# Second graph attention on four quarters of the matmul array, two tiles at a time, in a float32 GAT layer

## The chip, the cores and the metric

The kernel runs on one core of a Trainium2 chip. The metric is the device time of one execution in microseconds (us). I quote the median of a kernel's timed runs and, in brackets, the lowest and highest. A profile's span is some 2 us shorter than the device time of the same run, because it goes from the first to the last instruction.

Engines: PE is TensorE (matmul), PEld its weight loads, DVE VectorE, ACT ScalarE, POOL GpSimd, and SP SyncE, whose queue issues nearly all DMA transfers here. L272 means line 272 of that kernel's source.

## The reference

128 batches of 64 nodes with 512 features go through a graph attention layer with four heads, a second attention with one head, a feed-forward block and two norms. The part concerned here is the second attention and what follows it.

```python
def _gat_heads(x, adj, W, a):                     # x: [B, N, F]
    Wh = einsum('bnf,hfo->bhno', x, W)
    f1 = einsum('bhno,ho->bhn', Wh, a[:, :O])
    f2 = einsum('bhno,ho->bhn', Wh, a[:, O:])
    e = f1[:, :, :, None] + f2[:, :, None, :]
    e = where(e > 0, e, 0.01 * e)
    e = where(adj > 0, e, -1e9)
    return einsum('bhnm,bhmo->bhno', softmax(e), Wh)

# h = relu(layernorm(x)), then, with B = 128, N = 64, F = O = D = 512, H = 4:
h = elu(_gat_heads(h, adj, W_heads, a_heads))     # four heads, joined to [B, N, 2048]
out = elu(_gat_heads(h, adj, W_out, a_out))       # the second attention
y = maximum(out @ w1 + b1, 0) @ w2 + b2 + out
return x + layernorm(y) * gamma + beta
```

Each batch attends only within itself: the second attention is, for each batch, a 64x64 matrix times a 64x512 matrix.

## The kernel before

A tile is 128 partitions, that is two batches of 64 nodes, by 512 features. Four tiles form a group, and there are 16 groups. The large products run as seven half-size products each instead of eight (Strassen's scheme, in `unit`). Work of neighbouring groups is interleaved, so that TensorE always has a product to do. Cuts are marked with `# ...`.

The PSUM pools: six banks for products, two (`aux`) for everything else. The buffers for x tiles: four, shared by the x that the next group needs (`x`) and the x for the residual of a finished group (`xr`). Both are issued on the SP queue, as are the weights and the stores of results.

```python
    def bank(name):
        return ps.tile([P, 2, T], FP, tag="mm", name=name)        # 6 buffers

    def aux(shape, name):
        return ps.tile(shape, FP, tag="aux", name=name, bufs=2)

    def load(t, name="x"):
        tl = wk.tile([P, F], FP, tag="x", name=f"{name}{t}", bufs=4)
        nc.sync.dma_start(out=tl, in_=xf[ts(t, P), :])
        return tl
```

The second attention. `softmax2` leaves its weights as a block-diagonal 128x128 matrix for each tile (the two off-diagonal quarters are zero), so that one full matmul does both batches of a tile:

```python
    def transpose_weights2(g):
        # ... AT2[g][:, j, :] is the transposed block-diagonal matrix of tile j
    def attend2(g, j):
        pa = aux([P, FO], f"pa2_{g}_{j}")
        nc.tensor.matmul(pa, AT2[g][:, j, :], WH2[g][:, j, :], start=True, stop=True)
        # ...
        elu(OUT[g][:, j], pa, f"2_{g}_{j}")

    def elu(dst, src, name):
        ex = wk.tile([P, 512], FP, tag="elu", name=f"ex{name}", bufs=3)
        nc.scalar.activation(ex, src, AF.Relu, scale=-1.0)
        nc.scalar.activation(ex, ex, AF.Exp, scale=-1.0)
        nc.vector.scalar_tensor_tensor(dst, ex, -1.0, src, ALU.add, ALU.max)
```

The end of a tile's way: the residual is loaded, the norm taken, the result stored.

```python
        def finish(j):
            t = G * g + j
            xr = load(t, "xr")
            nc.gpsimd.tensor_tensor(xr, xr, bs, ALU.add)
            y = o[:, j]
            mean, rstd = norm_stats(y, "n2", t)
            nc.vector.scalar_tensor_tensor(y, y, mean, gs, ALU.subtract, ALU.mult)
            nc.vector.scalar_tensor_tensor(y, y, rstd, xr, ALU.mult, ALU.add)
            nc.sync.dma_start(out=of[ts(t, P), :], in_=y)
```

The seven products of a unit run in the order 1, 5, 6, 2, 3, 7, 4. Product 7 accumulates into the bank of product 6, so it may begin only when VectorE has added product 1 to that bank (L272) and ScalarE has copied the sum away (L273):

```python
        own = {1: 1, 2: 1, 5: 5, 3: 5, 6: 6, 7: 6, 4: 6}
        def after(p):
            if p in (1, 5, 6):
                nm = {1: "s1", 5: "s5", 6: "t"}[p]
                sb[nm] = wk.tile([P, 2, T], FP, tag=nm, name=f"{nm}_{name}")
                if p == 6:
                    nc.vector.tensor_tensor(gb[6], gb[6], sb["s1"], ALU.add)   # L272
                nc.scalar.copy(sb[nm], gb[p])                                  # L273
                # ...
```

And the first norm of a later group's tiles starts on VectorE with the statistics of x (L343), which have to wait for x's DMA:

```python
    def norm_stats(src, tag, t):
        st = sm.tile([P, 6], FP, tag=tag + "st", name=f"{tag}st{t}")
        nc.vector.bn_stats(st, src)                                            # L343
        # ...
    def norm1(t):
        if t not in X:
            X[t] = load(t)
        mean, rstd = norm_stats(X[t], "n1", t)
        # ...
```

## Time and profile before

| | before |
|---|---|
| device time, us | 2364.29 (2364.02 to 2364.80), 3 runs |
| length of each steady group, us | 142.96 |
| second attention on TensorE | 128 instructions of 592 ns, 0.86 us from start to start for a tile |
| SP queue's transfers of x, xr, results | 66, 64 and 64 of 256 KB |
| x, from issue to landing | 3.6 us (median) |

The prediction below shows the span, the busy times and the timeline of the second attention. First, what the SP queue issued around the start of a group (start in us, duration in us, queue, line, operation, destination<-source, count):

```profile
329.43 1.13 SPq L750 DMA_DIRECT2D out_dram<-o  x2
330.65 0.91 SPq L238 DMA_DIRECT2D w<-tc  x2
331.65 0.86 SPq L95 DMA_DIRECT2D x<-in_x_dram  x2
```

Read it as a queue: two stores, two weights, then two x tiles. The tiles' transfers landed at 335.25 and 335.94. Then the same moment on the engines (timeline of all engines, start in us, duration in us; in brackets the idle time before and what ended it):

```profile
335.57 1.28 DVE L343 BATCH_NORM_STATS2 n1st<-x 128x6 f32<-128x512 f32 x2
...
336.98 1.89 PE L307 MATMUL g_a<-zs_z,w 128*128 128x256 f32 x8
...
338.98 0.70 DVE L272 TENSOR_TENSOR g_a<-g_a,s_a 128x512 f32<-128x512 f32 x1 [1.72 <-PE g_a L307]
...
339.77 0.59 ACT L273 COPY t_a<-g_a 128x512 f32<-128x512 f32 x1 [1.95 <-DVE g_a L272]
```

The statistics of x were done by 336.9, before the sum of L272 was wanted: VectorE sat idle for 1.72 us ahead of it and then started the sum as soon as TensorE's product 6 was complete. Product 7 was not delayed. This group had the most room: over the twelve steady groups the idle time ahead of the sum was 0.14 to 1.72 us.

### The profile page before, as it was taken

How to read it: one execution, taken by the hardware profiler on the slowest of the kernel's cores; microseconds unless marked ns; L12 is line 12 of the kernel's file. 1: busy time of each engine (PE TensorE's matmuls, PEld its weight loads, DVE VectorE, ACT ScalarE, POOL GpSimd, SP SyncE). 2: the span in 40 equal slices, each digit the busy share in tenths (PEclk: the TensorE clock that was granted, in tenths of full speed). 3: DMA queues.
4: the chain of work that ended last, by engine and by line, in shares of the span. 5: the costliest groups of instructions: out<-in, count | busy, mean ns of one | idle time of the engine just before them, and what ended most of it. 6: DMA issues, size and time to landing. Idle time of an engine off the chain costs nothing.

```text
span 2360.4 us, 32849 instructions
## 1 busy us (share of the span) xinstructions
PE 2317.9 (98%) x11805; PEld 1934.5 (82%) x11805; DVE 1265.5 (54%) x2210; ACT 911.0 (39%) x1623; POOL 1026.7 (43%) x917
## 2 busy tenths in 40 slices
PE   6989999999999999999999999999999999999997
PEld 4868787888878888787887878888788887878885
DVE  7625474554646556474554745556464563744527
ACT  2524425253352533425244251533525344251513
POOL 5664444416344353443524444253443534533333
PEclk7999999999999999999999999999999999999999
DMA  8545353444535445353444544435354453534443
GB/s 308 184 142 193 125 183 127 164 152 132 182 125 178 134 139 179 126 180 129 154 163 129 182 131 161 153 130 181 127 177 132 138 179 127 182 118 164 157 148 106
DMA packets 257809, 366.89 MB, mean 155 GB/s; under 512 B 22216, under 2 KB 145128, under 8 KB 257648
## 3 DMA queue, kind: packets, MB, share of 16 engines
q1 hardware_dynamic: 251024, 343.82, 43.9%
q0 software_dynamic: 4512, 16.78, 1.9%
q10 hardware_dynamic: 2112, 4.19, 0.5%
q8 instruction: 95, 1.56, 0.3%
q14 instruction: 66, 0.54, 0.1%
HBM read 337.45 MB, written 27.26 MB: 155 GB/s over the span
## 4 chain that ended last, share of the span: by engine, by line
PE 94%; DVE 2%; ACT 1%; POOL 1%; issue 0%; DMA 0%; DVEq 0%
PE g_b L322 33%; PE g_a L307 32%; PE g_c L307 8%; PE g_d L322 8%; PE pz L525 4%; PE pa L673 2%; PE pto L700 1%; PE pzS L525 1%; PE pth L371 1%; PE s1pt L472 1%; PE pf L381 1%; PE s1pe L406 1%; DMA x<-in_x_dram 0%; PE s2pt L667 0%; PE pwa L193 0%
## 5 line engine op out<-in xcount | busy, mean ns | idle before, releaser
L322 PE MATMUL g_b<-w,h 128*128 128x256 f32 x2560 | 598.1, 381 | 0.0
L322 PEld LDWEIGHTS g_b<-w,h 128*128 128x128 f32 x2560 | 480.5, 190 | 72.2 <-issue 10.1
L307 PE MATMUL g_a<-z,w 128*128 128x256 f32 x1520 | 361.0, 380 | 1.2 <-DVE g_a L581 0.7
L307 PE MATMUL g_a<-zs_z,w 128*128 128x256 f32 x1504 | 347.9, 379 | 0.0
L307 PEld LDWEIGHTS g_a<-z,w 128*128 128x128 f32 x1520 | 287.6, 190 | 57.9 <-issue 14.3
L307 PEld LDWEIGHTS g_a<-zs_z,w 128*128 128x128 f32 x1504 | 284.8, 190 | 50.5 <-issue 14.3
L322 PE MATMUL g_b<-w,hS 128*128 128x256 f32 x1024 | 243.5, 382 | 0.0
L585 POOL TENSOR_TENSOR hS<-hS,h 128x512 f32<-128x512 f32 x64 | 83.0, 1297 | 366.8 <-DVE hS L549 366.8
L547 ACT ACTIVATE exc<-g_a 128x512 f32<-128x512 f32 x256 | 152.3, 595 | 199.7 <-DVE g_a L581 119.6
L322 PEld LDWEIGHTS g_b<-w,hS 128*128 128x128 f32 x1024 | 191.4, 191 | 30.9 <-issue 6.7
L549 DVE SCALAR_TENSOR_TENSOR h<-exc,g_a 128x512 f32<-128x512 f32 x192 | 131.6, 686 | 136.3 <-ACT exc L548 136.2
L548 ACT ACTIVATE exc<-exc 128x512 f32<-128x512 f32 x256 | 161.6, 631 | 6.5
L615 POOL TENSOR_TENSOR h<-h,h 128x512 f32<-128x512 f32 x64 | 86.7, 1362 | 138.1 <-PE g_b L322 138.0
L332 POOL TENSOR_TENSOR zs_z<-zS,z 128x512 f32<-128x512 f32 x63 | 89.7, 1424 | 128.3 <-PE g_a L307 123.7
L615 POOL TENSOR_TENSOR h<-hS,h 128x512 f32<-128x512 f32 x64 | 81.1, 1268 | 142.4 <-PE g_b L322 142.4
L474 ACT COPY at<-s1pt 128x512 f32<-128x512 f32 x64 | 34.7, 588 | 279.8 <-PE s1pt L472 279.8
L307 PE MATMUL g_c<-ot,w 128*128 128x256 f32 x512 | 123.9, 385 | 0.8 <-DVE n2ve L347 0.8
L322 PE MATMUL g_d<-w,rt 128*128 128x256 f32 x512 | 121.5, 380 | 1.7 <-DVE o L740 1.0
L307 PE MATMUL g_a<-zS,w 128*128 128x256 f32 x496 | 117.2, 379 | 0.0
L639 DVE SCALAR_TENSOR_TENSOR jf<-wh,ao 128x512 f32<-128x512 f32 x128 | 94.3, 776 | 40.3 <-ACT wh L621 40.1
L333 POOL TENSOR_TENSOR zs_z<-z,zs_z 128x512 f32<-128x512 f32 x63 | 85.4, 1357 | 61.1 <-PE g_a L307 40.7
L307 PEld LDWEIGHTS g_c<-ot,w 128*128 128x128 f32 x512 | 93.9, 190 | 21.8 <-issue 9.3
(159 smaller groups left out, 3535.6 us busy)
## 6 DMA issues: line engine op xcount, KB each, us to landing
w<-tc SPq DMA_DIRECT2D x632, 256.0 KB, 2.6
w<-in_L_gnn_W_heads_dram SPq DMA_DIRECT2D x192, 256.0 KB, 2.7
w<-in_L_gnn_W_out_dram SPq DMA_DIRECT2D x192, 256.0 KB, 2.7
w<-in_L_gnn_w_dram SPq DMA_DIRECT2D x96, 256.0 KB, 2.7
x<-in_x_dram SPq DMA_DIRECT2D x66, 256.0 KB, 3.6
xr<-in_x_dram SPq DMA_DIRECT2D x64, 256.0 KB, 2.8
out_dram<-o SPq DMA_DIRECT2D x64, 256.0 KB, 2.1
tc<-pt POOLq DMA_DIRECT2D x20, 512.0 KB, 5.6
```

Of the source, the lines that this page charges most:

```text
L307: nc.tensor.matmul(bk[:, o, :], w[:, k, ts(o, P)], a[:, k, :], start=start and o == 0 and k == 0, stop=k == 1, skip_group_check=True,)
L322: nc.tensor.matmul(bk[:, j, :], a[:, k, ts(j, P)], w[:, k, :], start=start and k == 0 and j == 0, stop=i == len(ms) - 1 and k == 1, skip_g ...
L332: eng.tensor_tensor(s2, s1, a11, ALU.subtract)
L333: eng.tensor_tensor(s4, a12, s2, ALU.subtract)
L525: nc.tensor.matmul(banks[b][:, c, :].rearrange("p (h n) -> p h n", h=H), src[rows, off + c * P:off + (c + 1) * P], at[rows, b], start=True ...
L547: nc.scalar.activation(ex, src, AF.Relu, scale=-1.0)
L548: nc.scalar.activation(ex, ex, AF.Exp, scale=-1.0)
L549: nc.vector.scalar_tensor_tensor(dst, ex, -1.0, src, ALU.add, ALU.max)
L585: nc.gpsimd.tensor_tensor(dst, dst, H1["22"][:, h], ALU.add)
L615: nc.gpsimd.tensor_tensor(dst[:, h], x0[:, h], x1[:, h], ALU.subtract)
L639: nc.vector.scalar_tensor_tensor(junk, WH2[g][:, j], 1.0, ao[:, c, :], ALU.mult, ALU.mult, accum_out=f[:, c, j:j + 1],)
L673: nc.tensor.matmul(pa, AT2[g][:, j, :], WH2[g][:, j, :], start=True, stop=True)
```

## The change

Half of each full matmul of the second attention multiplies zeros. The change uses only the two diagonal 64x64 quarters, and fills the other two quarters of the array with the second tile: four 64x64 matmuls, one for each of the four batches of two tiles, side by side. A row half of the array writes one PSUM bank, and a column half writes 64 partitions of it. So the results come out as tiles of other pairs of batches: one tile holds the first batch of both tiles, the next one the second batch of both. Everything after is per row and does not care, but the residual must be loaded and the result stored in two halves of 64 partitions (one batch, 128 KB, each), since the two batches of a tile are no longer neighbours in DRAM.

```diff
--- before.py
+++ after.py
@@ -668,22 +668,31 @@
         AT2[g] = wk.tile([P, G, P], FP, tag="hT", name=f"at2_{g}", bufs=4)
         nc.scalar.copy(AT2[g], pt)
 
-    def attend2(g, j):
-        pa = aux([P, FO], f"pa2_{g}_{j}")
-        nc.tensor.matmul(pa, AT2[g][:, j, :], WH2[g][:, j, :], start=True, stop=True)
-        if j == 0:
+    def attend2(g, q):
+
+
+        if q == 0:
             tag = "out" if g < NG - 1 else "z11"
             OUT[g] = big.tile([P, G, FO], FP, tag=tag, name=f"o{g}")
-        elu(OUT[g][:, j], pa, f"2_{g}_{j}")
+        pa = [aux([P, FO], f"pa2_{g}_{q}_{b}") for b in range(NB)]
+        for b in range(NB):
+            rows = slice(b * N, (b + 1) * N)
+            for c in range(2):
+                nc.tensor.matmul(
+                    pa[b][c * N:(c + 1) * N], AT2[g][rows, 2 * q + c, rows],
+                    WH2[g][rows, 2 * q + c, :], start=True, stop=True, skip_group_check=True,
+                )
+        for b in range(NB):
+            elu(OUT[g][:, 2 * q + b], pa[b], f"2_{g}_{q}_{b}")
 
     def stage_e(g):
 
         gap = [lambda: None]
         score = [lambda j=j: scores2(g, j) for j in range(G)]
-        attend = [lambda j=j: attend2(g, j) for j in range(G)]
+        attend = [lambda q=q: attend2(g, q) for q in range(2)]
         return (
             gap + score + [lambda: spread2(g)] + gap * 2 + [lambda: softmax2(g)] + gap * 5
-            + [lambda: transpose_weights2(g)] + gap * 2 + attend[0:2] + gap + attend[2:4] + gap * 3
+            + [lambda: transpose_weights2(g)] + gap * 2 + attend[0:1] + gap * 2 + attend[1:2] + gap * 4
         )
 
 
@@ -740,14 +749,18 @@
             eng.tensor_tensor(dst, a, dst, ALU.add)
 
         def finish(j):
-            t = G * g + j
-            xr = load(t, "xr")
+
+            batches = [NB * (G * g + j // 2 * 2 + c) + j % 2 for c in range(2)]
+            xr = wk.tile([P, F], FP, tag="x", name=f"xr{g}_{j}", bufs=4)
+            for c, b in enumerate(batches):
+                nc.sync.dma_start(out=xr[ts(c, N), :], in_=x[b])
             nc.gpsimd.tensor_tensor(xr, xr, bs, ALU.add)
             y = o[:, j]
-            mean, rstd = norm_stats(y, "n2", t)
+            mean, rstd = norm_stats(y, "n2", G * g + j)
             nc.vector.scalar_tensor_tensor(y, y, mean, gs, ALU.subtract, ALU.mult)
             nc.vector.scalar_tensor_tensor(y, y, rstd, xr, ALU.mult, ALU.add)
-            nc.sync.dma_start(out=of[ts(t, P), :], in_=y)
+            for c, b in enumerate(batches):
+                nc.sync.dma_start(out=out[b], in_=y[ts(c, N), :])
 
         f1 = unit(f"c{g}", product_t(M1, lambda p: bl[1][p]), post1, (1, 5, 6, 2, 3, 7, 4))
         f2 = unit(f"d{g}", product_n([M2], lambda p, i: bl[2][p]), post2, (1, 5, 6, 2, 3, 7, 4))
@@ -839,7 +852,7 @@
             run(ff[2:], [
                 lambda: [scores2(g, j) for j in range(G)], lambda: spread2(g), nothing, nothing,
                 lambda: softmax2(g), *[nothing] * 7, lambda: transpose_weights2(g), nothing,
-                *[lambda j=j: attend2(g, j) for j in range(G)], nothing,
+                *[lambda q=q: attend2(g, q) for q in range(2)], nothing,
             ])
             continue
         early = [lambda: z_sums(g + 1, 0)]
```

## The prediction

> **What bounds the kernel now.** I read the page's first, second and fourth parts, then the waits of TensorE inside the steady part, then the timelines around the second attention and the first attention's scores.
>
> The page: span, busy times, and the chain of work that ended last.
>
> ```profile
> span 2360.4 us, 32849 instructions
> PE 2317.9 (98%) x11805; PEld 1934.5 (82%) x11805; DVE 1265.5 (54%) x2210; ACT 911.0 (39%) x1623; POOL 1026.7 (43%) x917
> ...
> PEclk7999999999999999999999999999999999999999
> ...
> PE 94%; DVE 2%; ACT 1%; POOL 1%; issue 0%; DMA 0%; DVEq 0%
> ...
> PE g_b L322 33%; PE g_a L307 32%; PE g_c L307 8%; PE g_d L322 8%; PE pz L525 4%; PE pa L673 2%; PE pto L700 1%; PE pzS L525 1%; PE pth L371 1%; PE s1pt L472 1%; PE pf L381 1%; PE s1pe L406 1%; DMA x<-in_x_dram 0%; PE s2pt L667 0%; PE pwa L193 0%
> ```
>
> The reader is to see one engine only: TensorE is busy in 98% of the span at full clock and carries 94% of the chain. The waits of TensorE between 250 and 2290 us come back empty, so in fourteen of the sixteen groups of four tiles nothing else ends last. A group lasts 142.96 us (the second attention starts at 796.08 and again at 939.04). There, TensorE time saved is span saved, until something else makes TensorE wait. The changed line, pa at L673, is 2% of the chain: that caps the gain.
>
> The second attention of one group, on TensorE (start in us, length in us, ...). Lengths overlap at the ends; I use start to start.
>
> ```profile
> 937.32 1.89 PE L307 MATMUL g_a<-zs_z,w 128*128 128x256 f32 x8
> 939.04 1.02 PE L673 MATMUL pa<-wh,at 128*128 128x512 f32 x2
> 939.90 1.89 PE L307 MATMUL g_a<-zs_z,w 128*128 128x256 f32 x8
> 941.63 1.02 PE L673 MATMUL pa<-wh,at 128*128 128x512 f32 x2
> 942.49 1.89 PE L307 MATMUL g_a<-z,w 128*128 128x256 f32 x8
> ...
> 947.67 1.02 PE L673 MATMUL pa<-wh,at 128*128 128x512 f32 x2
> 948.53 1.89 PE L307 MATMUL g_a<-zs_z,w 128*128 128x256 f32 x8
> ```
>
> Each float32 matmul is two instructions. One tile's attention takes 939.90 - 939.04 = 0.86 us, i.e. 0.43 us for each 512-column instruction, and lies in the stream of products without any gap. The kernel already has a block of exactly the shape that the change makes, four matmuls on four quarters of the array: the scores of the first attention, 64*64 with 256 columns.
>
> ```profile
> 857.50 1.89 PE L322 MATMUL g_b<-w,h 128*128 128x256 f32 x8
> 859.23 1.89 PE L307 MATMUL g_c<-zs_o,w 128*128 128x256 f32 x8
> 860.95 1.89 PE L322 MATMUL g_b<-w,h 128*128 128x256 f32 x8
> 862.77 1.09 PE L406 MATMUL s1pe<-R,L 64*64 64x256 f32 x16
> 863.80 1.99 PE L307 MATMUL g_c<-ot,w 128*128 128x256 f32 x8
> 865.63 3.62 PE L322 MATMUL g_b<-w,h 128*128 128x256 f32 x16
> 869.08 1.24 PE L322 MATMUL g_d<-w,rt 128*128 128x256 f32 x5
> ```
>
> See that 16 quarter instructions take 1.03 us to the next start, where 16 whole ones take 3.45 (865.63 to 869.08): four run at once. See also what the switch costs: the 8 products ahead last 1.82 us instead of 1.73, and the 8 behind 1.83.
>
> **What the Trainium skill says.** "TensorEngine Tiling (Array Packing)", section Key Properties: tiles work in parallel, but a change of the tiling mode drains TensorE. The trace agrees, with the sum below at 0.37 us for in and out. The same page, Gotcha 1: PSUM Pressure: different row tiles must write to different PSUM banks. The change obeys this (one bank for each half of the rows), and so do the scores above. "TensorE: Matmul & The Clock Gate", Part 3, The mechanism: tiles' matmuls start about 4 ns apart; here the four starts of a set lie 6 to 8 ns apart, hidden all the same.
>
> **The change part by part.**
> 1. Removed from TensorE: 64 whole 128x512 matmuls, 0.86 us each (pa, 128 instructions), 55 us in all. They multiply a block-diagonal matrix whose off-diagonal halves are zero.
> 2. Added: 32 sets of four 64x64 matmuls with 512 columns (256 instructions, so TensorE should have 11,933). Half of a set's products were the zeros. Cost of a set, from the scores: from 860.95 to 865.63 are 4.68 us for 16 whole instructions and 16 quarter ones. Take off 3.45 for the whole ones: 1.23 us remain. Four sets of quarter instructions at the rate of one whole each (3.45/16 = 0.216) are 0.86, so **a switch in and out costs 0.37 us**. The set here has two passes of 512 columns: 2 x 0.43 = 0.86, plus 0.37, is **1.23 us** against 2 x 0.86 = 1.72 for the two tiles that it replaces. Saved: 0.49 us a set, x32 = **15.7 us**. All of it is on the path in the steady groups.
> 3. Unchanged: the ELUs. Two banks of 128x512 come out of a set as out of two tiles before, so 64 Relu of 0.59 us, 64 Exp of 0.63 and 64 VectorE operations of 0.69. Only which batches share a tile is new. ScalarE (39%) and VectorE (54%) keep their load.
> 4. Moved: a set takes both "aux" PSUM buffers at once. By the order of the built program, in a steady group set 1 stands where tile 0 stood, then come four blocks of 8 products (before: pa of tile 1 among them), then set 2, where tile 2 stood.
> 5. DMA: loads of xr and stores of the result become 128 of 128 KB each instead of 64 of 256 KB. Same bytes. Each issue takes the SP queue 0.34 us, so 128 more are 43 us over 2360, in a queue that mostly waits for TensorE to free weight buffers (L238, 655.4 + 529.4 us, the two lines below). Matching each weight load's landing in the trace with the first product that reads it gives 11.5 us at the least in the steady part, 16.3 in the median: hidden.
>
> ```profile
> SPq L238 <- PE g_a L307: 655.4, 434, 8.1
> SPq L238 <- PE g_b L322: 529.4, 371, 9.1
> ```
>
> 6. The tail, where TensorE does wait for others. In the last group the two sets are only one product block (1.73 us) apart, where tiles stood at 2309.69, 2312.28, 2314.86 and 2315.72. Set 2 needs both buffers, so it waits until both ELUs of set 1 are over: about 0.2 to land, then Relu, Exp, Relu, Exp = 2.44 on ScalarE, then 0.69 on VectorE, some 3.4 us from set 1's end, against 1.73. A stall of about 1.7 us. Of this, the later start of set 1 and the shorter sets give part back, and the old chain had its own wait (the fourth ELU ended at 2320.3). By laying these durations end to end I get the last transposed tile copied about 0.9 us later than before. The last store also has one issue more, 0.4 us. Sum: **+1.3 us** (estimate).
>
> Sum: 2364.3 - 15.7 + 1.3 = 2349.9, **2350 us**, a ratio of 1.006.
>
> **The rivals.**
> A. The PSUM buffers become the wait in every group: set 2 waits for set 1's ELUs. For: only two buffers, both taken at once, and ScalarE interleaves other ELUs (before, tile 0's ELU ran from 940.63 to 943.66 with the products' ELUs between). Against: set 2 would start at 939.04 + 1.23 + 4 x 1.73 = 947.2, and the two ELUs end, with the neighbours' work laid between, at about 944.5. Slack 2.6 us. If it did wait by 1 us in each group, the gain would be nil: 2366.
> B. The quarters don't overlap at 512 columns, or the two passes of one float32 matmul run one after another, making some five passes of 0.43 plus 0.37 = 2.5 us a set: +0.8 x 32 = +25, 2390. Against: the scores are issued in the same order (rows outer, columns inner) and overlap fully.
> C. The switch costs less with long passes, because the longer streaming hides the weight loads: at the best 0.86 us a set, -27 us, 2338. Against: half of the 0.37 (0.09 and 0.10) lies in the blocks ahead and behind, where longer passes hide nothing; that leaves some 6 us more at most.
> D. More, smaller DMAs delay weights or the store at the end. Against: 5. above; the worst I can see is 1 to 2 us at the end.
>
> **Range and chances.** The saving of 15.7 rests on a block of like shape measured in the same program, repeated to 0.01 us in each group; I allow it 13 to 18. The tail I allow 0 to 4. So 2345 to 2355. Faster by over 2% needs under 2318, more than all that pa costs less the floor of its passes (C: 2338): chance 0.01. Slower by over 2% needs 2412, beyond B: 0.01. Within 2%: 0.98.
>
> **What would show it right or wrong.** In the changed profile: pa as 64*64 x256; from one product block's start ahead of a set to the second behind it 1.23 us more than the blocks alone (2. right); a group of 141.97 us, 0.98 less than before; no TensorE waits between 250 and 2290 us (A, D wrong); mean length of the four ELU operations as before (3.); at the end one wait of TensorE's pa for VectorE of 1 to 2 us (6.). The prediction is wrong if a wait of pa for VectorE shows in every group (A), or weights' DMAs show as TensorE's releaser (D), or a set takes over 1.7 us (B).

## The result, and the profile after

| us | before | after |
|---|---|---|
| device time, median | 2364.23 (2364.02 to 2364.80), 4 runs | 2354.88 (2350.49 to 2357.07), 4 runs |
| ratio | | 0.9958 (0.994 to 0.9975) |
| device time of the profiled run | 2362.20 | 2357.07 |
| its span | 2360.4 | 2355.3 |

The ratio is the mean time of one kernel's fast runs over that of the other's in the same rounds, so it is not quite the ratio of the medians quoted. (The prediction's 1.006 is the other way round, before over after.) The time is 9.4 us shorter, within 2%; the range of 2345 to 2355 just holds it, but the prediction's middle was 2350.0. And the runs spread over 6.6 us, where those of before spread over 0.8. The profiled run after is the slowest of the four; the profiled run of before is a run apart, 2 us faster than the timed ones.

The page of the changed kernel, first part (span; busy time of each engine, share, instructions):

```profile
span 2355.3 us, 33359 instructions
PE 2306.5 (98%) x11933; PEld 1912.8 (81%) x11933; DVE 1273.8 (54%) x2210; ACT 910.2 (39%) x1623; POOL 1030.3 (44%) x917
```

TensorE lost 11.4 us of busy time, gained the 128 instructions that were expected (11,933), and is still the bound. The sets themselves, in the timeline of TensorE:

```profile
938.12 1.89 PE L307 MATMUL g_a<-zs_z,w 128*128 128x256 f32 x8
939.94 1.09 PE L681 MATMUL pa<-wh,at 64*64 64x512 f32 x8
940.96 1.99 PE L307 MATMUL g_a<-zs_z,w 128*128 128x256 f32 x8
942.79 1.89 PE L307 MATMUL g_a<-z,w 128*128 128x256 f32 x8
```

From 938.12 to 942.79 are 4.67 us; the two blocks of products take 1.73 each, so the set costs 1.22 us, where two tiles cost 1.72. The unrounded starts give 1.217 us for each of the 30 sets outside the last group. A steady group, with two sets, should therefore have shrunk from 142.96 to 141.96 us. To see whether it did, I took the distance between the scores blocks of neighbouring groups. Twelve steady groups have 142.96 us each before. After, they have between 142.02 and 143.19, and their sum is 1711.0 against 1715.5 before and 1703.5 expected: **7.5 us of the 12.0 were lost again**. The waits of TensorE between 250 and 2280 us, a question that had an empty answer before, name where (engine, tile, line, what it waited for: us in total, times, longest):

```profile
PE g_a L307 <- ACT t_a L273: 4.5, 7, 1.0
```

The view counts only idle time that it can see, 4.5 us. The whole 7.5 can be placed with a later run, e5, which has the same 11,933 TensorE instructions in the same order and no such wait: matched instruction by instruction between 250 and 2280 us, all of the extra time (7.4 us) lies ahead of the first two instructions of product 7 of the first head, in each of the twelve groups.

Here is one of these seven, in the timeline of all engines:

```profile
340.91 0.70 DVE L343 BATCH_NORM_STATS2 n1st<-x 128x6 f32<-128x512 f32 x1 [4.25 <-DMA x<-in_x_dram]
...
341.43 1.89 PE L307 MATMUL g_a<-zs_z,w 128*128 128x256 f32 x8
...
341.74 0.66 DVE L343 BATCH_NORM_STATS2 n1st<-x 128x6 f32<-128x512 f32 x1
...
342.73 0.70 DVE L272 TENSOR_TENSOR g_a<-g_a,s_a 128x512 f32<-128x512 f32 x1
...
343.52 0.58 ACT L273 COPY t_a<-g_a 128x512 f32<-128x512 f32 x1 [4.70 <-DVE g_a L272]
...
344.16 0.70 PE L307 MATMUL g_a<-zs_z,w 128*128 128x256 f32 x2 [0.84 <-ACT t_a L273]
```

Read it from the bottom. TensorE stood 0.84 us (product 7 of the first head) for ScalarE's copy, ScalarE for VectorE's sum of L272. VectorE was not waiting for anything just before that sum: it was busy with the statistics of x, which stand ahead of it in its queue and which it had begun only at 340.91, after 4.25 us of waiting for the DMA of x. Before, those statistics were over in time. So the engine named by the wait, ScalarE, is two steps away from the cause. The SP queue shows why x was late:

```profile
331.36 2.42 SPq L763 DMA_DIRECT2D out_dram<-o  x4
333.88 1.30 SPq L238 DMA_DIRECT2D w<-tc  x2
335.28 0.38 SPq L238 DMA_DIRECT2D w<-in_L_gnn_W_heads_dram  x1
335.75 0.89 SPq L95 DMA_DIRECT2D x<-in_x_dram  x2
```

TensorE is 1.0 us later here than before (this run started 2.0 us slower, see below, and one group's sets have saved 1.0). The first store was issued 1.93 us later than before, but the first x load 4.10 us later. The four halves of stores take 2.42 us where the two whole stores took 1.13, and one weight load more stands ahead of x. The tiles' landing, at 340.88 and 341.56, also came 5.1 to 5.3 us after their issue against 3.6 to 3.8 before. Over the whole run, x takes longer from issue to landing (median 3.6 before, 4.1 after), and VectorE's wait for x rose from 110.9 to 153.5 us. Neither total is a measure of the loss, as the experiments show: e5 has 3.9 and loses nothing, e7 waits 151.0 us and loses in one group only.

How late the sum of L272 is decides it. Counted from the scores block of its group, it starts at 48.05 us in every steady group before, and 1.7 to 2.9 us later in every one after. Each group's loss is that lateness less 1.64 us, to within 0.01 us, in all twelve groups: so long a delay is hidden by the products between the sum and product 7, and the rest is paid.

One issue of a half takes the SP queue 0.57 us for stores and 0.55 for residuals (medians of 128 each); whole tiles took 0.34 and 0.38 before.

The tail was expected to hold a wait for the two `aux` buffers. TensorE's timeline of the last group's second set:

```profile
2309.14 1.08 PE L681 MATMUL pa<-wh,at 64*64 64x512 f32 x4
2310.46 1.07 PE L681 MATMUL pa<-wh,at 64*64 64x512 f32 x4 [0.24 <-DVE o L549]
2311.46 1.99 PE L322 MATMUL g_d<-w,rt 128*128 128x256 f32 x8
```

The set came apart by itself: the four instructions that write the first bank went ahead, and the other four waited for the second bank's ELU. The view shows 0.24 us of idle time, because the long overlapping instructions count as busy. From start to start, the set takes 2.32 us to the next block, where one in a steady group takes 1.02: a stall of 1.3 us.

The end of the last VectorE operation and the end of the span lie 3.27 us apart before (2357.15 and 2360.42) and 4.73 after (2350.56 and 2355.30): storing in halves costs 1.5 us at the end.

The first stretches of the program, before any changed instruction, are 2.0 us longer in this profiled run than in that of before: 0.6 us to the first scores block, and 0.7 in each of the next two stretches. They vary by run (the first stretch between scores blocks took 44.9 to 47.9 us over the profiles), and I ascribe them to no part of the change. The page's chain of work broke off near the end of the program in this run, so I don't use it.

### The profile page after: what moved, and what is told of

Read it like the earlier page. It is cut to its first block, busy times and chain, and to the rows that moved or that the text cites. A ratio compares the mean times of both kernels' runs of the same rounds, so it can differ in the third digit from the quotient of the medians.

```text
span 2355.3 us, 33359 instructions
## 1 busy us (share of the span) xinstructions
PE 2306.5 (98%) x11933; PEld 1912.8 (81%) x11933; DVE 1273.8 (54%) x2210; ACT 910.2 (39%) x1623; POOL 1030.3 (44%) x917
## 5 line engine op out<-in xcount | busy, mean ns | idle before, releaser
L307 PE MATMUL g_a<-zs_z,w 128*128 128x256 f32 x1504 | 353.7, 382 | 4.7 <-ACT t_a L273 4.5
L343 DVE BATCH_NORM_STATS2 n1st<-x 128x6 f32<-128x512 f32 x64 | 43.8, 687 | 153.5 <-DMA x<-in_x_dram 153.5
L757 POOL TENSOR_TENSOR xr<-xr,bs 128x512 f32<-128x512 f32 x64 | 89.6, 1402 | 76.1 <-DMA xr<-in_x_dram 48.6
```

The lines of the kernel that those rows point to most:

```text
L307: nc.tensor.matmul(bk[:, o, :], w[:, k, ts(o, P)], a[:, k, :], start=start and o == 0 and k == 0, stop=k == 1, skip_group_check=True,)
```

## The experiments

**The theory (D')**: the sets save what was predicted. Splitting residual loads and stores in halves makes the SP queue late with x, so the statistics of x stand in VectorE's queue when the sum for product 7 is wanted. **The rivals**: the sets themselves disturb the start of a group (other times of the ELUs, both `aux` buffers taken at once), or the loss comes from other work that has moved; then removing the half transfers would not help. Ten kernels were run. Ratios are against the kernel before in the same rounds.

### e1_merged, e3_loads_merged, e4_stores_merged: one transfer for both halves

The changed kernel, with each pair of halves as one DMA over a strided view. e3 does this for the loads alone, e4 for the stores alone.

```diff
-            for c, b in enumerate(batches):
-                nc.sync.dma_start(out=xr[ts(c, N), :], in_=x[b])
+            nc.sync.dma_start(
+                out=xr, in_=x.rearrange("(u c b) n f -> u b c n f", c=2, b=NB)[G // 2 * g + j // 2, j % 2]
+            )
```

> The changed kernel, with each xr load and each store of a result as one transfer of 256 KB over two batches that lie two apart (a strided view of x and out) instead of two of 128 KB. TensorE's and ScalarE's order is that of the changed kernel, line for line; results stay right. Theory D' (the doubled small transfers make the loads of x land later, VectorE's batch statistics wait for them, and the sum g_a+s_a, ScalarE's copy t_a and a TensorE product queue up behind): 2348 to 2350.5 us, no wait of TensorE for ScalarE t_a between 250 and 2280 us, every steady group 141.97 us, spread of runs under 1 us. Rival S (the sets themselves, their ELUs or the PSUM buffers cost the missing time): 2353 to 2357, the t_a waits stay.

> The changed kernel with only the xr loads merged; stores stay split. Theory D': part of the lost time comes back; the four store halves just ahead of the loads of x in the SP queue are the nearer cause, so most waits stay: 2351 to 2355. If loads are the cause: 2349 to 2351.

> The changed kernel with only the stores merged; xr loads stay split. Theory D' with the stores as the nearer cause: 2348.5 to 2351, few or no t_a waits. If loads are the cause: 2353 to 2356.

Measured: e1 2717.9 us (2715.8 to 2719.4), ratio 1.1492; e3 2469.1, ratio 1.0441; e4 2563.5, ratio 1.0841. All three missed their expectation by far (e1 is 353 us slower than the kernel before), and they do not test the question. In e1 the first residual was issued at 263.8 and its reader on GpSimd began at 272.2, 8.4 us later, where a whole tile takes 2.8 from issue to landing before. GpSimd waited 456 us for residuals, and a group took about 165 us. The Trainium skill, "DMA: Bandwidth & Descriptors", section "Why a DMA increments its semaphore by 16 and not by 1", under "How many engines (k)", gives a reason: the number of DMA engines used is the largest one up to 16 that divides the slowest dimension, larger than 1, of both access patterns. My view has a slowest dimension of 2, so it would run on two engines of sixteen. The kept trace of e1 agrees: the semaphore of that first residual got three updates, one 1.0 us after the issue began and two at 272.04 and 272.06, when it landed (one from each engine, as I read it). The same load in the kernel before got sixteen, all at its landing. The largest waits of TensorE in e1 (same question as above; 250 to 2280 us is less of this longer program):

```profile
PE s1pt L472 <- DVE s1A L439: 167.4, 12, 14.2
PE g_a L307 <- ACT t_a L273: 60.4, 12, 5.5
```

The second line is the same wait as in the changed kernel, thirteen times as long in total. Late transfers can reach TensorE by this way, then; by how much the halves do it needs cleaner experiments.

### e2_before_split: the half transfers alone, on the kernel before

Each residual and each result of the kernel before goes in two halves. Nothing else moves: TensorE and ScalarE have the instructions of before in the same order.

```diff
-            xr = load(t, "xr")
+            xr = wk.tile([P, F], FP, tag="x", name=f"xr{t}", bufs=4)
+            for c in range(2):
+                nc.sync.dma_start(out=xr[ts(c, N), :], in_=x[NB * t + c])
...
-            nc.sync.dma_start(out=of[ts(t, P), :], in_=y)
+            for c in range(2):
+                nc.sync.dma_start(out=out[NB * t + c], in_=y[ts(c, N), :])
```

> The kernel before, with only its xr loads and result stores split in two halves of 128 KB (by batches). TensorE's and ScalarE's order is that of the kernel before. Theory D': t_a waits of TensorE appear here too, 2366 to 2372 us (0.2 to 0.6 us in each of twelve groups, plus about 0.4 at the end), and runs spread by some us. Rival S: as before, 2364 to 2365, no waits.

Measured: 2373.9 us (2370.8 to 2375.4), ratio 1.0037. The steady groups grew from 142.96 to between 143.0 and 144.75 us, and the wait that was new after the change is there too, without any set on quarters:

```profile
PE g_a L307 <- ACT t_a L273: 7.6, 9, 1.5
```

The half transfers alone cost 9 us here, a little more than expected. This rules out that the sets are needed for the wait. Matched with the kernel before, instruction by instruction, all of TensorE's extra time between 250 and 2280 us (10.6 us in the profiled run) again lies at product 7.

### e5_old_transfers: the sets alone (wrong results on purpose)

The changed kernel with the transfers of before: each tile loads and stores the two batches that it would have held before. The results are wrong (half the batches land in each other's place); the work on every engine is that of the changed kernel.

```diff
-            batches = [NB * (G * g + j // 2 * 2 + c) + j % 2 for c in range(2)]
-            xr = wk.tile([P, F], FP, tag="x", name=f"xr{g}_{j}", bufs=4)
-            for c, b in enumerate(batches):
-                nc.sync.dma_start(out=xr[ts(c, N), :], in_=x[b])
+            t = G * g + j
+            xr = load(t, "xr")
...
-            for c, b in enumerate(batches):
-                nc.sync.dma_start(out=out[b], in_=y[ts(c, N), :])
+            nc.sync.dma_start(out=of[ts(t, P), :], in_=y)
```

> Wrong results on purpose: the changed kernel with the old xr loads and stores (one transfer of 256 KB over 128 neighbouring rows, so tiles go to the wrong rows and get the wrong residual). TensorE's and ScalarE's order is that of the changed kernel line for line, the SP queue's order that of the kernel before. It isolates the sets from the transfers. Theory D' (the doubled transfers cost the missing time): 2348 to 2350.5 us, no TensorE wait for t_a between 250 and 2280 us, steady group 141.97 us, runs within 1 us of each other. Rival S (the sets, ELUs or PSUM buffers): 2353 to 2357.

Measured: 2349.26 us (2348.58 to 2351.57), ratio 0.9936. All twelve steady groups take 141.96 us, and the question for TensorE's waits between 250 and 2280 us has an empty answer again. VectorE waits 113.1 us for x, as before. So the whole loss is in the transfers, and the sets alone give very nearly what was predicted. At the end of the program, the last VectorE operation and the end of the span are 3.27 us apart, as in the kernel before.

### e6_pairs, e7_store_pairs: halves of two tiles in one transfer

With two tiles done, 64 partitions hold two batches that are neighbours in DRAM, so a transfer of 64 partitions can take 2 x 2 KB from each, 256 KB in all. That brings the number of transfers back to that of before with correct results. e6 does it for loads and stores (x buffers come in pairs for it), e7 for the stores only.

```diff
-            for c, b in enumerate(batches):
-                nc.sync.dma_start(out=out[b], in_=y[ts(c, N), :])
+            if j % 2:
+                for c in range(2):
+                    t = G * g + j // 2 * 2 + c
+                    nc.sync.dma_start(
+                        out=out[NB * t:NB * (t + 1)].rearrange("b n f -> n b f"), in_=o[ts(c, N), j - 1:j + 1]
+                    )
```

> Right results: the changed kernel with the two tiles of a set loaded and stored together, as two transfers of 64 partitions x 2 x 2 KB (256 KB each, number as in the kernel before); x tiles lie in pairs too, so the buffers are the same size but are freed two at a time. Theory D': 2348.5 to 2352 us, t_a waits gone or nearly, issue-to-landing of x near 3.6 us. If it is the shape of the transfer (64 partitions) and not the number: 2353 to 2357. Risk: buffers freed in pairs make x loads wait.

> Right results: the changed kernel with only the stores in pairs (two of 64 x 2 x 2 KB for two tiles); the xr loads stay 128 of 128 KB. Theory D', stores just ahead of the x loads being the nearer cause: 2349 to 2352. If the split loads weigh as much: 2352 to 2355.

Measured: e7 2350.33 us (2348.86 to 2355.92), ratio 0.9942. Eleven steady groups take 141.96 us and one 143.44. So changing the stores alone removes nearly all of the loss. It changes more than their number: the first of a group's two x loads now goes out ahead of the stores, 38.6 us after the group's scores block (median) instead of 43.3, and two paired stores take 1.35 us where four halves took 2.42 (at 331.67 and 331.36). Which of the two helps more was not tried. e6 missed: 2364.20 us (2362.38 to 2366.06), ratio 0.9998. The wait is there, in 12 groups:

```profile
PE g_a L311 <- ACT t_a L277: 10.2, 12, 1.4
```

In e6 a residual lands 4.4 us after its issue (2.7 after the change), VectorE waits for residuals in the step before the stores (for 1.16 us at 323.57, for example), and x buffers come free two at a time. The two x loads go out 45.1 and 46.1 us after the scores block, later than in the changed kernel, and the sum of L272 is 3.0 to 4.0 us late. So e6 loses by the same late x; that the paired buffers make it late is read from the trace and not tried by itself, so that part is argued, not shown.

### e8_x_on_act: x tiles issued on another queue

The changed kernel with its half transfers, but the x tiles from the fourth group on are issued by ScalarE's queue, so that they no longer stand behind the SP queue's stores and weights.

```diff
-        nc.sync.dma_start(out=tl, in_=xf[ts(t, P), :])
+        (nc.scalar if t >= 3 * G else nc.sync).dma_start(out=tl, in_=xf[ts(t, P), :])
```

> Right results: the changed kernel with all its split transfers, but the prefetched x tiles (from tile 12) are issued from ScalarE's queue instead of SP's, so they don't stand behind the stores and weights. Theory D' in its narrow form (what counts is when x is issued, behind four stores in the SP queue): x lands earlier, VectorE's wait on x falls below the 111 us of the kernel before, t_a waits vanish: 2348.5 to 2352. If the load on the transfer engines counts and not the queue's order: 2353 to 2357.

Measured: 2342.96 us (2342.78 to 2346.61), ratio 0.9911, correct. All steady groups take 141.96 us, TensorE has no waits there, and x takes 2.9 us from issue to landing. One expected sign missed: VectorE's wait for x is 118.5 us in total, not below 111. VectorE's timeline at the same place in the program:

```profile
329.57 0.69 DVE L343 BATCH_NORM_STATS2 n1st<-x 128x6 f32<-128x512 f32 x1 [0.39 <-DMA x<-in_x_dram]
...
333.49 0.70 DVE L272 TENSOR_TENSOR g_a<-g_a,s_a 128x512 f32<-128x512 f32 x1 [1.60 <-PE g_a L307]
```

The statistics are done 3 us before the sum, which waits for TensorE again and not the other way round. The half transfers are all still there, so with x out of their queue their work on the DMA engines costs TensorE nothing. (x also goes out earlier here, at 39.2 us after the scores block against 40.7 before, so how much of the slower landing after, 5.0 against 4.1 us in the steady groups, is the halves' work on the DMA engines stays open.) The Trainium skill, "DMA: Bandwidth & Descriptors", section "Rules for kernel authors", says that spreading transfers over issuing engines gives no bandwidth and only saves the issuing sequencer's time; this run agrees that such time can be worth having.

It was 6 us better than expected. The surplus has a place: the stretch from the second to the third scores block takes 78.96 us instead of 83.77 before. That stretch holds no set, which suggested a wait for x that the kernel before had all along. (The next expectation calls it the stretch from the first to the second block; it is the second to the third.)

The runs side by side, over the twelve steady groups, all in us. The issue of the group's two x loads is a median and counts from the group's scores block; "late" is against 48.05 us after that block; lost time is against 142.96 with the old attention and 141.96 with the sets:

| run | x loads issued | sum of L272 late by | lost in a group |
|---|---|---|---|
| before, e5 | 40.7 and 41.2 | 0 | 0 |
| after | 43.3 and 43.8 | 1.7 to 2.9 | 0.06 to 1.23 |
| e2 | 43.7 and 44.2 | 1.7 to 3.4 | 0.04 to 1.79 |
| e6 | 45.1 and 46.1 | 3.0 to 4.0 | 1.38 to 2.32 |
| e7 | 38.6 and 43.3 | 0.4 to 1.3, once 3.1 | 0, once 1.48 |
| e8 | 39.2 and 40.0 | 0 | 0 |

In every row, a group loses only when the sum is more than 1.64 to 1.66 us late, and then it loses the excess.

### e9_before_x_on_act: the same edit on the kernel before

The edit is that of e8, to the kernel before. It does more here: in the kernel before, `load` also fetches the residuals, so those from tile 12 on moved to ScalarE's queue as well, which neither this heading nor the expectation says. From the page of e9:

```profile
xr<-in_x_dram ACTq DMA_DIRECT2D x52, 256.0 KB, 3.4
```

> The kernel before, with only the x tiles from tile 12 on issued from ScalarE's queue instead of SP's. TensorE's order is that of the kernel before. The run with the same edit on the changed kernel came out at 2343.0, some 6 us under the sets' own 2349, with the stretch from the first to the second scores block 4.8 us shorter than before. Theory: those 5 us have nothing to do with the sets (a late x held up VectorE near the start in the kernel before too): 2358 to 2360.5 us, steady group 142.96, the sets' gain on top of it again 15 to 16.5. Rival: the 5 us come from sets and queue together: 2363 to 2365.

Measured: 2359.78 us (2358.48 to 2360.63), ratio 0.9982. The steady groups stay at 142.96 us, and the early stretch is 78.68. So some 5 us were an old late x near the start: in that stretch only x loads had moved, the first moved residual being that of the fourth group. Between e9 and e8, where TensorE waits for nothing in the steady groups, lie 16.8 us. It is only a rough check of the worth of the sets, since the residuals stand in different queues, e8 alone stores in halves at the end (1.5 us), and the two ran in different rounds.

### e10_sets_adjacent: both sets of a group back to back

e8, and both sets of a steady group follow each other directly; the second one takes two banks of the products' pool. The last group is unchanged.

```diff
-    def attend2(g, q):
+    def attend2(g, qs):
...
-        pa = [aux([P, FO], f"pa2_{g}_{q}_{b}") for b in range(NB)]
+        pa = {}
+        for i, q in enumerate(qs):
+            for b in range(NB):
+                if i == 0:
+                    pa[q, b] = aux([P, FO], f"pa2_{g}_{q}_{b}")
+                else:
+                    pa[q, b] = bank(f"pa2_{g}_{q}_{b}").rearrange("p a b -> p (a b)")
...
-            + [lambda: transpose_weights2(g)] + gap * 2 + attend[0:1] + gap * 2 + attend[1:2] + gap * 4
+            + [lambda: transpose_weights2(g)] + gap * 2 + attend + gap * 7
```

> The changed kernel with x on ScalarE's queue, and the two sets of each steady group put next to each other (the second in two banks of the products' pool), so that the array is switched in and out once a group instead of twice. It measures the switch: if the 0.37 us are paid for each switch and not for each set, TensorE saves 0.37 in each of 15 groups and the run is 2337 to 2338.5 us, steady group 141.59. Rival: the second set's banks or the eight ELU operations in a row hold up the next products' copies s_a on ScalarE, TensorE waits 0.5 to 2 us a group: 2343 to 2365.

Measured: 2337.50 us (2336.09 to 2339.09), ratio 0.9888, correct: the best of all. A steady group takes 141.61 us. TensorE's timeline:

```profile
927.27 1.89 PE L307 MATMUL g_a<-zs_z,w 128*128 128x256 f32 x8
929.09 1.95 PE L688 MATMUL pa<-wh,at 64*64 64x512 f32 x16
930.97 1.99 PE L307 MATMUL g_a<-zs_z,w 128*128 128x256 f32 x8
932.80 1.46 PE L307 MATMUL g_a<-z,w 128*128 128x256 f32 x6
```

From 927.27 to 932.80 are 5.53 us. Less two blocks of 1.73, two sets cost 2.07, and four passes of 0.43 are 1.72: one switch in and out of 0.35 us for both. So the 0.37 us is a cost of the switch, here paid once for two sets. Rival C's hope of hiding it does not hold, but it can be halved. The eight ELU operations did not hold anything up: TensorE has no waits between 250 and 2280 us.

## Why the prediction was right or wrong

Within 2% was right, and the median lies at the very edge of the range, 4.9 us above its middle. By its own steps:

1. **Removed, and 2. a set costs 1.23 us**: right to about 0.01 us. Measured 1.217 net; 32 x (1.716 - 1.217) = 16.0 us against 15.7. e5 carries it on the clock: with the old transfers the sets save 15.1 us against the kernel before in the same rounds.
3. **The ELUs unchanged**: right. Relu 590 and 587 ns, Exp 638 and 630, VectorE 685 and 683, before and after.
4. **Both `aux` buffers at once, with slack in the steady groups** (rival A): right. In the group shown, the second ELU ended at 945.06 and the second set began at 948.07: 3.0 us of slack, 2.6 predicted. TensorE waited for these buffers only in the last group (step 6).
5. **"Same bytes. Each issue takes the SP queue 0.34 us ... hidden"**: this is the step that failed, in three ways. An issue of a half takes 0.55 to 0.57 us, so splitting a store lengthens its issue from 0.34 to 1.14 us (two medians added). The prediction's size came from the issue of a whole tile, and half the bytes were taken not to cost more. Then it measured the slack of the weights (11.5 us at the least, by its own matching, which shows in no view) and concluded for the queue, but it never measured x: before, the statistics of x were over 0.14 to 1.72 us before the sum of L272, and that sum could be another 1.64 us late unnoticed. And the wait does not show as a DMA: it reaches TensorE over VectorE's order and a ScalarE copy. It cost 7.5 us in the steady groups of the profiled run, where the prediction had 0; e2 and e5 show it from both sides, e8 removes it with correct results and e7 nearly so. Rival D was the right rival with the wrong victim, "weights or the store at the end", and with 1 to 2 us it was too small.
6. **The tail, +1.3**: nearly right in size, by terms that cancel. In that step's sum the last two sets had already been credited with 1.0 in step 2. From the block ahead of the last group's first set to the end, before takes 50.73 us (from 2309.69) and after 51.14 (from 2304.16 on, one block of products having moved ahead of the set): +0.4, or +1.4 net of the credit. The stall of 1.7 us came, as 1.3, with each half of the set waiting for its own bank only. The end's stores cost 1.5 us instead of 0.4. That these two did not add up to more is due to waits that the kernel before had in its tail and this one has not, such as 1.35 us for `zs_o` at 2327.65; which of the changes freed them was not looked into.

Rival B (no overlap) is refuted by each set; rival C (a cheaper switch) too: the long passes hid none of it.

Sum, from profiled run to profiled run: 2362.2 + 2.0 (start) - 16.0 + 1.4 + 7.5 = 2357.1, and 2357.07 were measured. What differs between the four runs after, 2350.5 to 2357.1, I take to be how late x lands in each and how slowly each starts; only one of them was profiled, so this stays open. That the median fell just inside the range owes something to luck: the three slowest of the four runs are 2353.7, 2356.0 and 2357.1, two of them outside. The profile before had one warning that was not used: in one steady group the statistics of x were over only 0.14 us before the sum. The total of VectorE's waits for x was no such sign, since e8 has more of it (118.5 us against 110.9) and loses nothing.

The Trainium skill would have helped with step 5: "DMA: Bandwidth & Descriptors", section "Rules for kernel authors", advises against two transfers to disjoint halves of the partitions in favour of one over 128. The runs agree with the advice: e2 against the kernel before is 9 us for nothing else. The cost found here, the longer issue ahead of x, is not the reason that the page gives.

## What to carry to other kernels

Measure the slack of every load in a queue, not of the most frequent one: added issues delay whatever stands behind them, and an engine that works in order and waits for a late tile passes the delay on to work that has nothing to do with that tile. When a change alters a layout, count its transfers at the issue time of their own shape, and give the most urgent load a queue of its own. Quarter-array matmuls paid here even at 0.37 us for each switch, and more when sets were put side by side.

## What the Trainium skill lacked or had wrong

- "TensorEngine Tiling (Array Packing)", section Key Properties, says that a change of tiling mode drains TensorE but gives no figure. Here: 0.36 to 0.37 us in and out for a single set, and 0.35 once for two adjacent sets.
- "TensorE: Matmul & The Clock Gate", Part 3, The mechanism: starts of side-by-side tiles about 4 ns apart. Here 64x64 tiles in float32 start 6 to 7 ns apart. It made no difference to the cost of a set (1.22 us).
- The same page, section "LDWEIGHTS (loading the stationary operand)", gives columns / 1.2 ns without a word on the data type: 53 for 64 columns and 107 for 128. In float32 here: 131 ns (129 to 133) and 190 ns, by median.
- No page that I found gives the SP queue's time for one issue on this chip by the shape of the transfer. Here, by median: 0.34 to 0.38 us for 128 partitions of 2 KB, 0.55 to 0.59 us for 64 partitions of 2 KB, 0.63 to 0.65 for 64 partitions of 2 x 2 KB, and 0.56 to 0.58 for 128 partitions in the strided views of e1, e3 and e4. Half the bytes took longer to issue; the reason stays open.
